# Values of the eleventh of sixteen groups of the second attention, projected between the FFN's gated product and its last product

## The chip, the cores and the metric

The kernel runs on one core of one Trainium2 chip. The metric is the device time of one execution in microseconds (us). The five engines of the core have queues of their own: PE (matrix products; PEld are its weight loads), DVE, ACT and POOL (elementwise work), and SP, which here only issues transfers (DMAs). An engine takes its instructions in the order in which the program has them. [...]

## What is computed

Four layers, each with a normalisation before it and a residual sum after it, on x of 32 sequences of 128 tokens with 256 features, all in float32:

```python
x = x + xattn_0(layernorm(x), ctx, ctx, mask)          # 16 heads of 16, masked
x = x + ffn_0(layernorm(x), w_gate, w_up, w_down)      # fake-quantised, 768 wide
x = x + xattn_1(layernorm(x), ctx, ctx, Wq, ..., beta) # 16 heads of 64
x = x + moe(layernorm(x), W1, b1, W2, b2, Wr, br)      # 8 experts of 1024, one per token
```

In the second layer every quantisation takes its scale from the largest magnitude of a whole tensor, so a step can't begin before the step ahead of it has ended for all tokens:

```python
x = act_qdq(x)
up = act_qdq(x @ lpbq_dequant(w_up).T)
gate = act_qdq(x @ lpbq_dequant(w_gate).T)
sig = fixed_qdq_u16(sigmoid(gate))
gate = act_qdq(gate * sig)
o = act_qdq(gate * up)            # the gated product
return o @ lpbq_dequant(w_down).T # the last product
```

In the third layer the values depend on the context alone, not on the layers before it:

```python
v = (value @ Wv + bv).reshape(b, value.shape[1], N_HEAD, VALUE_DIM)
out = einsum('bhqk,bkhd->bqhd', softmax(q k / 8), v)
```

## The kernel before

The tokens stand as 32 blocks of 128 (one sequence each). The stages follow each other: first attention, FFN, second attention, experts. Most stages are written with an order by hand: PE, DVE, ACT and POOL run their instructions as the source issues them; SP's order is the tile framework's, which also puts in every wait and decides from which instruction on a buffer is free.

*The second attention* goes through 16 groups of two blocks (G = 2). Each block has two units of eight heads, so a group is four units u = 0 to 3, and the loop over n runs 64 units. While unit n's probabilities are transposed (`transpose_c`, L1094) and multiplied by the values (`values_c`, L1109), unit n+1's scores are made (`scores_c`, L1052), and between these PE does the steps of the next group (`step`, L1000 and L1019): eight steps for its keys and queries, and four more for its values, two halves of 512 columns for each of two blocks. The constant NF (10) says for how many groups the values have been made beforehand. For such a group `values_of` (L1031) loads them from a DRAM tensor `v_d` with one transfer of 1024 KB. In the unit loop, `short = g + 1 < NF` chooses between two orders by hand: the short one issues eight steps over the four units of group g, the other one twelve (three per unit). So the units of groups 0 to 8 have the short order and those of groups 9 to 15 the long one.

*The values made beforehand.* These projections are set into the FFN, where PE has idle time. The pool `vf` holds the weights `wv_f` and three buffers `cf` for a block's transposed context (`load_v`, L678, 128 KB each from `ct_d`). `project_v(b, h, ps)` (L685) makes half h of block b with two matmuls of 512 columns (four records in the trace); `take_v` (L692, L693) copies the PSUM bank to a buffer `vs` and SP writes it to `v_d` (256 KB). Blocks 0 and 1 are made in the loop of up-projections. Then comes the gated product: a loop over 16 half-tiles s, with two ACT passes (L815, L818) and two DVE passes (L821, and `absmax` at L596) each, in which PE makes blocks 2 to 17; their banks are taken one round later. After this loop block 17 is taken, and the last loop (L826) makes blocks 18 and 19, both copied by ACT. The PSUM banks of this stage rotate over six, the buffers `vs` over five.

*Then the last product.* The global maximum is reduced (DVE L144, POOL L146), the scales s_o and k_o are worked out (DVE L834 to L839), and `quant_o(n)` quantises two blocks at a time: DVE makes int16 (L1245), ACT turns them back to float32 `oq` (L1247), and PE multiplies by `wdT` (L1265), 24 records in each of 16 rounds. After a round DVE adds x1, which SP has read back from DRAM (L1254, two buffers), and SP writes the sum x2 (L1272). `quant_o(n + 2)` stands ahead of round n's sum on DVE. SP also loads the weights of the attention here (L1277, L1279, 1024 KB each), and ACT issues the loads of small rows and biases (L857 to L870). The pools of this stage use space that the pools `vf` and `vp` (of `vs`) held.

Of the kernel before, what the change touches and what calls it, by code (L numbers as in the profile page):

```python
# [36 lines left out]
def tile_xattn_ffn_d2(  # L37
# [67 lines left out]
    toks_d = dram.tile([NC * P, 1], F32, name="toks_d")  # L105
    kacc_d = dram.tile([E, D], F32, name="kacc_d")

    NF = 10
    G = 2
    TG = G * P  # L110
    v_d = dram.tile([NF * G, P, D1], F32, name="v_d")

# [88 lines left out]
    with (  # L201
# [323 lines left out]
        with tc.manual_schedule(engines=by_hand):  # L525
            for n in range(-9, N + 8):
                b, k = divmod(n, KD)
# [67 lines left out]
    def absmax(n, t, i, r):  # L595
        nc.vector.tensor_reduce(  # L596
            amax[n][:, t, i : i + 1], r, AX.XY, ALU.max, apply_absolute_value=True
        )
# [4 lines left out]
    def half(r, i):  # L603
        return r[:, i * HM : (i + 1) * HM, :]
# [72 lines left out]
    def load_v(b):  # L677
        if b < NF * G:  # L678
            cfs[b] = vf.tile([P, KD, P], F32, tag="cf", name="cf", bufs=3)
            nc.sync.dma_start(out=cfs[b], in_=ct_d[b])  # L680

    def project_v(b, h, ps):

        for k in range(KD):
            nc.tensor.matmul(  # L685
                ps, lhsT=cfs[b][:, k, :], rhs=wv_f[:, k, h * 512 : (h + 1) * 512],
                start=(k == 0), stop=(k == KD - 1),
            )

    def take_v(b, h, ps, pool, copy):  # L690
        vs = pool.tile([P, 512], F32, tag="vs", name="vs")
        copy(vs, ps)  # L692
        nc.sync.dma_start(out=v_d[b, :, h * 512 : (h + 1) * 512], in_=vs)  # L693
# [3 lines left out]
    with (  # L697
# [44 lines left out]
        for t in range(NT):  # L742
# [5 lines left out]
            if t % 2:  # L748
                b, h = divmod(t // 2, 2)
# [25 lines left out]
    with (  # L775
        tc.tile_pool(name="bq", bufs=2, side="left") as ql,
        tc.tile_pool(name="ub", bufs=5, side="right") as ub,
        tc.tile_pool(name="vp", bufs=5, side="right") as vp,
        tc.tile_pool(name="b_v", bufs=6, space=PSUM) as pv,
        tc.manual_schedule(engines=by_hand),  # L780
    ):
        order = [*range(NT * 2 - KEPT, NT * 2), *range(NT * 2 - KEPT)]
        FU = 5

        def load_u(s):
            if s < NT * 2 and order[s] < NT * 2 - KEPT:
                n = order[s]
                ups[divmod(n, 2)] = ub.tile([P, HM, TB], F32, tag="ub", name="ub", bufs=FU)
                nc.sync.dma_start(
                    out=ups[divmod(n, 2)], in_=u_d[n].rearrange("p (m b) -> p m b", m=HM)  # L790
                )

        for s in range(KEPT + FU - 1):
            load_u(s)

        def take(s, h):

            if took:
                copy = nc.vector.tensor_copy if h and s % 2 else nc.scalar.copy
                take_v(1 + s, h, took[h], vp, copy)  # L800

        taken = []
        for s, n in enumerate(order):
            took, taken = taken, []
            for h in range(2):
                taken.append(pv.tile([P, 512], F32, tag="v", name="ps_vf"))
                project_v(2 + s, h, taken[h])
            load_v(5 + s)
            if s >= KEPT:
                load_u(s + FU - 1)  # L810
            t, i = divmod(n, 2)
            r = half(gates[t], i)
            u = ups[t, i]
            u16 = ql.tile([P, HM, TB], I16, tag="u16", name="u16")
            nc.scalar.activation(u16, u, AF.Copy, scale=i_u)  # L815
            take(s, 0)
            gs16 = ql.tile([P, HM, TB], I16, tag="gs16", name="gs16")
            nc.scalar.activation(gs16, r, AF.Copy, scale=k_s)  # L818
            take(s, 1)

            nc.vector.scalar_tensor_tensor(r, gs16, s_s, u16, ALU.mult, ALU.mult)  # L821
            absmax("o", t, i, r)
        took = taken
        for h in range(2):
            take(NT * 2, h)
        for b in range(2 + NT * 2, NF * G):  # L826
            for h in range(2):
                ps_v = pv.tile([P, 512], F32, tag="v", name="ps_vf")
                project_v(b, h, ps_v)
                take_v(b, h, ps_v, vp, nc.scalar.copy)  # L830
# [155 lines left out]
    def step(g, n):  # L986
# [3 lines left out]
        if "kT" not in s:  # L990
            if g >= NF:
                s["v"] = qkv.tile([P, G, D1], F32, tag="v", name="v")
# [36 lines left out]
    def values_of(g):  # L1029

        if g < NF:  # L1031
            groups_[g]["v"] = qkv.tile([P, G, D1], F32, tag="v", name="v")
# [541 lines left out]
    with tc.manual_schedule(engines=by_hand):  # L1574
# [16 lines left out]
        for n in range(N):  # L1591
            b, hf = divmod(n, 2)
# [4 lines left out]

            short = g + 1 < NF
            if short:
# [284 lines left out]
```

## Time and profile before

| | us |
|---|---|
| median of three runs (lowest, highest) | 1555.7 (1555.5, 1561.92) |
| the profiled execution: its time | 1557.21 |
| the profiled execution: span from first to last instruction | 1555.5 |
| mean granted clock of PE in it | 0.992 |
| gated product and values, from the last up-projection to PE's last projection | about 465 to 532.15 |
| last product of the FFN on PE | 538.73 to 624.18 |
| second attention, steps and units | 624.18 to about 1245 |
| experts | to 1555.5 |

The page gives busy times over the whole span. What a change in one stage is worth is read from that stage: from the order of events around it, and from the busy time of each engine in a stretch. Times in the trace count from the start of the span. Two kinds of idle time matter here: of PE between two products, and of a queue that waits for a transfer to land.

### The profile page before, as it was taken

Reading aid. Unit: us, or ns where it says so; the run is one execution under the profiler, and the core shown is the slowest. Engines: PE = TensorE matmul, PEld = TensorE weight load, DVE = VectorE, ACT = ScalarE, POOL = GpSimd, SP = SyncE. Lnnn points to the kernel's source line nnn. Section 1 sums busy time; section 2 is a strip of 40 time slices with the busy share of each in tenths; the row PEclk is TensorE's granted clock in tenths of the full one; section 3 lists DMA queues with packets and bytes.
Section 4 is the critical chain, followed back from the end, with each engine's and each line's share of the span. In section 5 each row is a group of like instructions: output and inputs, shape, how many; then the busy total and the mean of one; then the engine's idle time right before and its main releaser. Section 6 shows DMA issues by size and latency. Waiting matters only on the chain. (4 is left out here: it accounts for less than half of the span.)

```text
span 1555.5 us, 27850 instructions
## 1 busy us (share of the span) xinstructions
PE 1495.8 (96%) x9912; PEld 1109.1 (71%) x9912; DVE 945.6 (61%) x2290; ACT 821.3 (53%) x2425; POOL 455.5 (29%) x529
## 2 busy tenths in 40 slices
PE   8999999899998799999999999999999998999996
PEld 5656566444443388788888888777777667999996
DVE  7999998345999834456666666656566551333332
ACT  6878787345989732465566555454544421111111
POOL 6656664000000001223333333323233222232221
PEclk9999999999999999999999999999999999999998
DMA  7222211001437875213222321010102235251430
GB/s 242 69 86 83 66 35 46 14 5 74 159 123 257 292 206 168 85 55 55 55 55 56 60 59 60 16 26 23 21 19 64 55 106 202 101 170 50 166 104 12
DMA packets 84172, 139.99 MB, mean 90 GB/s; under 512 B 13098, under 2 KB 61245, under 8 KB 80448
## 3 DMA queue, kind: packets, MB, share of 16 engines
q1 hardware_dynamic: 74496, 125.16, 25.2%
q0 software_dynamic: 5568, 12.61, 2.8%
q8 instruction: 80, 1.31, 0.4%
q10 hardware_dynamic: 3968, 0.42, 0.4%
q14 instruction: 60, 0.49, 0.2%
HBM read 147.53 MB, written 45.77 MB: 124 GB/s over the span
## 5 line engine op out<-in xcount | busy, mean ns | idle before, releaser
L1071 ACT ACTIVATE pr_c<-sc_c,nmaxc 128x128 f32<-128x128 f32 x512 | 183.2, 384 | 194.1 <-DVE nmaxc L1062 137.9
L1083 POOL TENSOR_TENSOR pr_c<-pr_c,rsumc 128x512 f32<-128x512 f32 x64 | 92.8, 1449 | 279.4 <-DVE rsumc L1080 226.6
L1444 ACT ACTIVATE hT<-h_ps,w1s 128x128 f32<-128x128 f32 x156 | 48.1, 365 | 221.7 <-issue 141.5
L1010 DVE TENSOR_SCALAR qT<-ps_qk,bqk 128x256 f32<-128x256 f32 x128 | 61.8, 483 | 136.3 <-ACT kT L1006 135.6
L419 ACT ACTIVATE pr<-sc_a,nmaxa 128x128 f32<-128x128 f32 x512 | 140.1, 399 | 3.5 <-DVE nmaxa L410 3.5
L1000 PE MATMUL ps_qk<-cT,wk_s 128*128 128x256 f32 x512 | 140.3, 396 | 0.0
L1476 PE MATMUL y_d<-w2s,hT 128*128 128x256 f32 x576 | 133.3, 385 | 4.3 <-ACT hT L1444 4.3
L1435 PEld LDWEIGHTS h_ps<-xbT,w1s 128*128 128x128 f32 x1152 | 134.1, 192 | 1.7
L1435 PE MATMUL h_ps<-xbT,w1s 128*128 128x128 f32 x1152 | 134.6, 275 | 0.0
L1000 PE MATMUL ps_qk<-rT,wq_s 128*128 128x256 f32 x512 | 131.4, 379 | 0.0
L1476 PEld LDWEIGHTS y_d<-w2s,hT 128*128 128x128 f32 x576 | 108.7, 194 | 18.4 <-ACT hT L1444 4.5
L1122 PE MATMUL y_ps<-wo_s,oT 128*128 128x256 f32 x512 | 117.0, 382 | 0.0
L1071 ACT ACTIVATION_READ_ACCUMULATOR pr_c<-sc_c,nmaxc 128x1 f32 x512 | 114.0, 223 | 0.0
L1446 DVE TENSOR_SCALAR hT<-h_ps,w1s 128x128 f32<-128x128 f32 x132 | 40.1, 346 | 110.1 <-ACT hT L1444 110.1
L1000 PEld LDWEIGHTS ps_qk<-rT,wq_s 128*128 128x128 f32 x512 | 97.3, 190 | 13.2
L1122 PEld LDWEIGHTS y_ps<-wo_s,oT 128*128 128x128 f32 x512 | 94.7, 190 | 12.0 <-DVE pid L1721 0.4
L1000 PEld LDWEIGHTS ps_qk<-cT,wk_s 128*128 128x128 f32 x512 | 87.4, 189 | 18.8 <-issue 5.1
L1006 ACT ACTIVATE kT<-ps_qk,bqk 128x256 f32<-128x256 f32 x128 | 63.6, 498 | 57.4 <-PE ps_qk L1000 57.4
L1265 PE MATMUL ps_dn<-wdT,oq 128*128 128x256 f32 x384 | 85.1, 384 | 6.6 <-ACT oq L1247 6.6
L410 DVE TENSOR_REDUCE nmaxa<-sc_a 128x4 f32<-128x512 f32 x128 | 82.1, 683 | 11.6 <-PE sc_a L401 11.4
L1265 PEld LDWEIGHTS ps_dn<-wdT,oq 128*128 128x128 f32 x384 | 74.0, 193 | 17.7 <-ACT oq L1247 7.4
L609 PE MATMUL ps_mm<-xqT,wgT 128*128 128x512 f32 x192 | 83.8, 593 | 0.2 <-ACT xqT L641 0.2
(279 smaller groups left out, 2983.4 us busy)
## 6 DMA issues: line engine op xcount, KB each, us to landing
w1s<-in_W1b_dram SPq DMA_DIRECT2D x34, 1028.0 KB
w2s<-in_W_dram SPq DMA_DIRECT2D x34, 1024.0 KB
v_d<-vs SPq DMA_DIRECT2D x40, 256.0 KB
v<-v_d SPq DMA_DIRECT2D x10, 1024.0 KB
u_d<-u SPq DMA_DIRECT2D x12, 768.0 KB
ub<-u_d SPq DMA_DIRECT2D x12, 768.0 KB
w2e<-in_W_dram SPq DMA_DIRECT2D x8, 1024.0 KB
rows_d<-row SPq DMA_DIRECT2D x32, 256.0 KB
```

Of the source, the lines that this page charges most:

```text
L410: nc.vector.tensor_reduce(u["nmax"][:, r, :], u["scs"][r], AX.X, ALU.max, negate=True)
L419: nc.scalar.activation(u["pr"][:, r * HQ + j, :], u["scs"][r][:, j, :], AF.Exp, bias=u["nmax"][:, r, j : j + 1],)
L609: nc.tensor.matmul(ps, lhsT=wT[:, k, m * P : (m + 1) * P], rhs=xqT[:, k, t * TB : (t + 1) * TB], start=(k == 0), stop=(k == KD - 1),)
L1000: nc.tensor.matmul(ps[:, j, :], lhsT=w_[:, k, m * P : (m + 1) * P], rhs=src[:, k, :], start=(k == 0), stop=(k == KD - 1),)
L1006: nc.scalar.activation(s["kT"][:, m, :], ps[:, 0, :], AF.Identity, bias=bqk[:, 1, m : m + 1])
L1010: nc.vector.tensor_scalar(s["qT"][:, m, :], ps[:, 1, :], bqk[:, 0, m : m + 1], HD1**-0.5, ALU.add, ALU.mult,)
L1071: nc.scalar.activation(u["pr"][:, h, :], u["scs"][par][:, mm, :], AF.Exp, bias=u["nmax"][par][:, mm : mm + 1], accum_out=u["sums"][:, h : ...
L1083: eng.tensor_tensor(pr[:, j : j + 4, :], pr[:, j : j + 4, :], bc(rsum[:, j : j + 4], 2, P), ALU.mult,)
L1122: nc.tensor.matmul(t["y_ps"][:, :D], lhsT=t["oT"][:, m, :], rhs=wo_s[:, m, :], start=(m == 0), stop=(m == M1 - 1),)
L1265: nc.tensor.matmul(ps[:, j, :], lhsT=oq[:, m, j * P : (j + 1) * P], rhs=wdT[:, m, :], start=(m == 0), stop=(m == M0 - 1),)
L1435: nc.tensor.matmul(h_ps[:, c4, :], lhsT=wb[:, k * FF + c * P : k * FF + (c + 1) * P], rhs=xbT[:, k, :], start=(k == 0), stop=(k == KD - 1),)
L1476: nc.tensor.matmul(y_ps[:, :D], lhsT=hT[:, c, :], rhs=w2t[:, c, :], start=(c == 0), stop=(c == MF - 1),)
```

## The change

NF goes from 10 to 11. So the tensor `v_d` has 22 blocks, the last loop of the stage makes blocks 18 to 21 instead of 18 and 19, `values_of` loads group 10 from DRAM too, and the units of group 9, in which group 10 is prepared, have the short order. As blocks 20 and 21 have to be loaded, the loop over s loads block 20 in its last round (there `load_v(5 + s)` did nothing before, since 20 was no block to be made), and the last loop calls `load_v(b + 3)`, which loads block 21 while b is 18 and does nothing after that. Block 21 takes the buffer of block 18, and its transfer waits for that block's last matmul.

```diff
-    NF = 10
+    NF = 11
     G = 2
     TG = G * P
     v_d = dram.tile([NF * G, P, D1], F32, name="v_d")
...
         for h in range(2):
             take(NT * 2, h)
         for b in range(2 + NT * 2, NF * G):
+            load_v(b + 3)
             for h in range(2):
                 ps_v = pv.tile([P, 512], F32, tag="v", name="ps_vf")
                 project_v(b, h, ps_v)
                 take_v(b, h, ps_v, vp, nc.scalar.copy)
```

In the changed program every line from L827 on stands one lower.

## The prediction

> **What bounds the kernel now.** The page's first part says that PE is the engine to look at; it does not say where its free time is.
>
> ```profile
> PE 1495.8 (96%) x9912; PEld 1109.1 (71%) x9912; DVE 945.6 (61%) x2290; ACT 821.3 (53%) x2425; POOL 455.5 (29%) x529
> ```
>
> So I read two stages: the one that gives work away and the one that takes it. First the attention, by stretches that run from one group's second score product to the next group's (columns: stretch, its length, then PE, PEld, DVE, ACT, POOL busy, PE's clock, DMA share, GB/s).
>
> ```profile
> 893.51:929.92 36.41, 36.19 (x278) 30.63 (x277) 23.74 (x75) 22.06 (x86) 13.37 (x14) 1.00 0.24 60
> 929.92:966.32 36.40, 36.19 (x277) 30.61 (x277) 23.57 (x74) 21.84 (x86) 13.34 (x13) 1.00 0.27 56
> 966.32:1009.86 43.54, 43.32 (x293) 33.28 (x292) 26.98 (x82) 21.96 (x87) 15.26 (x15) 1.00 0.09 25
> 1009.86:1052.86 43.00, 43.00 (x293) 33.28 (x292) 26.10 (x79) 21.58 (x86) 13.25 (x13) 1.00 0.11 26
> 1052.86:1095.86 43.00, 43.00 (x293) 33.28 (x292) 26.11 (x79) 21.48 (x86) 12.96 (x13) 1.00 0.11 26
> ```
>
> A short group takes 36.4 us, a long one 43.0 (the first long one 43.54). PE is full in both, the others are not and the DMAs have room, so a group's length is its PE work. Here PE work that goes away is time that goes away.
>
> Then the timeline of PE, DVE and ACT where the FFN's last product begins.
>
> ```profile
> 518.13 14.02 PE L685 MATMUL ps_vf<-wv_f,cf 128*128 128x512 f32 x32 [0.66 <-DMA cf<-ct_d]
> 538.73 61.44 PE L1265 MATMUL ps_dn<-wdT,oq 128*128 128x256 f32 x276 [6.58 <-ACT oq L1247]
> ...
> 535.76 0.16 DVE L839 TENSOR_TENSOR k_o<-i_o,s_u 128x1 f32<-128x1 f32 x1
> 536.04 1.95 DVE L1245 TENSOR_SCALAR o<-r,k_o 128x1536 int16<-128x1536 f32 x2
> ...
> 531.25 0.59 ACT L692 COPY vs<-ps_vf 128x512 f32<-128x512 f32 x1 [0.67 <-DMA v_d<-vs]
> 533.18 0.59 ACT L692 COPY vs<-ps_vf 128x512 f32<-128x512 f32 x1 [1.34 <-DMA v_d<-vs]
> 537.10 1.57 ACT L1247 ACTIVATE oq<-o,s_o 128x1536 f32<-128x1536 int16 x1 [3.34 <-DVE o L1245]
> ```
>
> PE ends block 19 at 532.15 and then has nothing for 6.58 us, until the maximum, the scales, the int16 pass (1.0 us of the 1.95 for two) and oq (1.57) are done. The clock pays for this idle time:
>
> ```profile
> 532.15:538.73 6.58, 0.01 (x1) 0.01 (x1) 5.09 (x10) 2.22 (x3) 0.55 (x2) 0.73 0.90 304
> 538.73:545.81 7.08, 7.08 (x25) 6.00 (x26) 1.00 (x1) 1.41 (x1) 0.01 (x1) 0.77 0.90 299
> 545.81:550.99 5.18, 5.18 (x25) 4.56 (x24) 1.62 (x2) 1.57 (x1) 0.00 (x0) 1.00 0.81 49
> ```
>
> The first round of the last product takes 7.08 us at a clock of 0.77, the next one 5.18 at 1.00: 1.90 us lost. So this hole costs 6.58 of idle time and 1.90 behind it.
>
> **The change part by part.**
>
> *Removed from the attention.* The units of group 9 go from the long order to the short one: 43.00 - 36.41 = **6.59 us** off PE's path. The 0.54 us by which the first long group is longer goes along to group 10 and is no gain. Checked from the other side: four value steps are 16 records, and 32 records took 14.02 us, so 16 take 7.01; the short order gives 0.4 of it back. I take 6.59, bounds 6.59 to 7.01. The four DVE copies that go too are worth nothing beside a full PE. Added: one load of 1024 KB from v_d by SP while group 9 runs, as for groups 1 to 9; in those stretches the DMAs are a quarter busy, and the load has a group's 36 us to land. I cost it at nothing; were it late, unit 40's value product would wait for it.
>
> *Added to the FFN: PE.* Blocks 20 and 21 are four half projections of 1.75 us (14.02 / 8), 7.01 us, right behind block 19: from 532.15 to 539.16, if nothing holds them up. What could: (a) Their context. SP loads block 20 when block 17 is made (eight halves run from 518.13, so 17 ends at 525.1), block 21 when block 18 is made (528.6); each has 7 us until it is used, and the worst load here was used 7.6 us after its issue, 0.66 late, while 768 KB reads ran beside it, of which none are left now. (b) PSUM: with six banks, block 20's first half takes the bank of block 17's first half, which ACT emptied at 528.55 to 529.1. (c) The copies. With five vs buffers a copy waits until the write five before it has landed: 531.25 and 533.18 are such waits, each about 2.1 us after SP's issue of that write (529.15, 531.02). The next writes are issued from 531.43 to 532.92, some 0.5 us apart; at 2.1 us plus a backlog of 0.3 us for each (256 KB take about 0.8 us at 340 GB/s, an estimate from the 304 GB/s of the stretch above at its share of 0.90) they land between 533.6 and 536.5. PE ends the four halves at 533.9, 535.7, 537.4 and 539.2, so copies wait for PE and not the reverse.
>
> *The wait that comes in its place.* In the order of the changed program the first int16 pass (DVE, L1246 there) has a wait for PE, as it has before: its tile lies in space of the pool of the projections, so it waits for the last of them. Before, that was over at 532.15, nearly four us ahead of k_o. Now it ends at 539.16, three us behind k_o (535.92). Behind this instruction stand the second int16 pass and then everything of DVE; ACT has only the last copy (539.2 to 539.8) ahead of oq. So: int16 539.25 to 540.25, oq 540.3 to 541.87, first matmul of the last product at about 541.9 in place of 538.73: **+3.2 us**. PE's hole shrinks from 6.58 to 2.7 us.
>
> *The clock.* The trace has two other holes of that size: 2.69 us ahead of the transposes at 642.14, and 2.50 at 475.37. Stretches 639 to 642 and 642 to 646 both show a clock of 1.00. Only the holes of 6.58 and of 4.31 us (ahead of 1304.17) show it at half. So I take it as kept: **-1.9 us**; bounds -1.9 and 0.
>
> *Added: DMAs.* Four writes of 256 KB and two loads of 128 KB on SP's queue, 1.25 MB, about 3.9 us at 340 GB/s. Queued behind them are the attention's weights: the first waited until 538.38 for all writes of v_d, and now waits until about 542.6 (last copy 539.8, then a write). ACT's bias loads wait for the same. They are needed at 624 only, but the sums of x1 stand among them:
>
> ```profile
> SPq L1277 <- DMA bqk<-in_L_xattn_bq_dram: 8.1, 1, 8.1
> ...
> 561.55 0.69 DVE L1271 TENSOR_TENSOR x1r<-ps_dn,x1r 128x512 f32<-128x512 f32 x1 [8.94 <-PE ps_dn L1265]
> ...
> 563.26 1.57 ACT L1247 ACTIVATE oq<-o,s_o 128x1536 f32<-128x1536 int16 x1 [5.52 <-DVE o L1245]
> ```
>
> The line names PE, but round 2's matmuls had ended at 556.2: the sum waited five us more for x1, which SP issued at 556.50. The int16 pass for round 5 stands behind it, so oq(5) was ready at 564.83, and PE needed it at 538.73 + 7.08 + 4 x 5.18 = 566.5: 1.7 us of cover. In the changed program SP writes the first x2 ahead of the third weight, not behind it, and reads x1 back ahead of the last weight. Both ends: all of it 4.2 us later against a PE 1.3 us later eats the cover and stalls PE by 4.2 - 1.3 - 1.7 = 1.2 us; the new order takes 1024 KB (3 us) out of the way twice and stalls nothing. I take 0, bounds 0 and 1.2.
>
> *Sum.* -6.6 + 3.2 - 1.9 = **-5.3 us** on a span of 1555.5: 1550.2. The profiled execution took 1557.21, 1.7 more than its span, which would be 1551.9; the median of the runs, 1555.7, is 1.5 below that execution, and becomes **1550.4**.
>
> **The rivals.**
>
> *A, the clock is lost again.* The mean clock is 0.52 in 535 to 540 and 0.80 in 540 to 545, so it was at half from 535.2 to 542.0; 0.53 in 1303 to 1306 and 0.60 in 1306 to 1311 put the second such time at 1303.2 to 1310.0. It fell 3.0 and 3.3 us into the holes. For: 2.7 is only 0.3 short of that. Against: the two holes of 2.5 and 2.7. Then the 1.9 isn't won: 1552.3.
>
> *B, the clock is won elsewhere too.* Ahead of the experts PE is idle from 1299.86 to 1304.17, the clock fell at 1303.2, and 16 records took 6.59 us that take 3.45 at 5.18 / 24 each: 3.1 us. Both half-speed times last 6.8 us and their starts are 768 us apart, which is 112.5 times 6.83: all four edges lie on a grid of 3.41 us. If the clock is judged on that grid, the hole held nearly a whole step (1299.8 to 1303.2); 5.3 us earlier, from 1294.6 to 1298.9, the edge at 1296.4 cuts it into 1.8 and 2.5, and the clock stays. Time 1550.4 - 3.1 = 1547.3. Against: if the fall just follows 3.0 to 3.3 us of idle time, nothing changes. [...]
>
> *C, slower: the chain through x2 and x1.* An x1 buffer is read again only when its x2 has landed: 547.82 to 556.50 to 561.55, 13.7 us, where two rounds of PE take 10.4. With 1.25 MB more ahead of it and bias loads that held SP's queue for 8.1 us, round 2's sum may come so late that PE is paced by transfers. It decides from a landing at 564.5 on (561.55 + 1.7 + 1.3), and the kernel is slower than before from 569.8 on. At a landing 12 us later than before (573.5) the stall is 9 us: 1559.4. For: 0.8 to 1.0 DMA share from 532 to 560. Against: the new order of SP's queue.
>
> *D, the attention gives nothing back,* because the short order was fast only beside early groups: 1555.7 + 1.3 = 1557.0. Against: nine groups run it at the same length.
>
> **How the numbers follow.** Forecast 0.52, A 0.15, B 0.20, C 0.08, D 0.05. What a measurement here tells from no change is about 0.5%, 7.8 us: faster is below 1547.9, slower above 1563.5. B is faster (0.20), and a little of the forecast with the 7.01 and a lucky clock (0.03): 0.23. Slower needs C at twice the price worked out or something unseen: 0.06. The rest, 0.71, is the same. The range: below, 1555.7 - 7.0 - 1.9 + 3.2 - 3.1 = 1546.9; above, A with the stall of 1.2 is 1553.5, and up to C's beginning 1555.
>
> **What would show it.** Right: group 9's stretch at 36.4 us; eight halves and then four more on PE without a gap, the first L1266 matmul at 541 to 543, released by oq, its first round at 5.2 us and a clock of 1.00; round 2's sum before 564. Wrong: a hole of over 3.4 us ahead of the last product, a wait of PE for oq in its rounds 3 to 8, or a group 9 longer than 37 us.

## The result, and the profile after

| | before | after |
|---|---|---|
| median of 20 runs each, us | 1559.09 | 1555.61 |
| lowest to highest, us | 1555.5 to 1563.14 | 1553.3 to 1558.16 |
| the profiled execution: time, span, us | 1557.21, 1555.5 | 1556.43, 1554.7 |

The ratio is 0.9979 (95% interval 0.9972 to 0.9986): the changed kernel is 3.3 us faster (2.2 to 4.4), about 0.2%. The forecast was 1550.4, a gain of 5.3. The three runs of before that it started from had their median at 1555.7; 20 runs have it at 1559.09. So of the 5.2 us between 1550.4 and 1555.6 some 3 are the starting point, and 2 are the size of the change. The kernel scatters by 7.6 us from run to run; the last point of the causes below says what that is seen to come from.

The attention first. These stretches of the changed kernel run from one group's second score product to the next group's, as those shown of before: their length, then PE, PEld, DVE, ACT, POOL busy, PE's clock, DMA share, GB/s.

```profile
937.40:973.81 36.41, 36.19 (x278) 30.62 (x277) 23.58 (x74) 21.85 (x86) 13.34 (x13) 1.00 0.34 59
973.81:1010.22 36.41, 36.19 (x278) 30.62 (x277) 23.82 (x75) 22.06 (x86) 13.40 (x14) 1.00 0.21 57
1010.22:1053.76 43.54, 43.32 (x294) 33.27 (x293) 26.91 (x82) 21.96 (x87) 15.23 (x15) 1.00 0.12 26
```

The stretch in the middle, the changed one, took 43.54 before; the first long group, 43.54, is now one later, where 43.00 stood. The scores of unit 37 start 7.49 us later than before (973.81 against 966.32), those of unit 45 only 0.90 (1053.76 against 1052.86): 6.59 us are gone, the forecast's figure to the digit.

Then the timeline of PE, DVE and ACT around the start of the FFN's last product.

```profile
524.53 15.72 PE L685 MATMUL ps_vf<-wv_f,cf 128*128 128x512 f32 x36 [0.46 <-ACT vs L692]
537.19 0.16 DVE L840 TENSOR_TENSOR k_o<-i_o,s_u 128x1 f32<-128x1 f32 x1
540.29 1.95 DVE L1246 TENSOR_SCALAR o<-r,k_o 128x1536 int16<-128x1536 f32 x2 [2.94 <-PE ps_vf L685]
541.34 3.04 ACT L1248 ACTIVATE oq<-o,s_o 128x1536 f32<-128x1536 int16 x2 [0.42 <-DVE o L1246]
542.97 64.11 PE L1266 MATMUL ps_dn<-wdT,oq 128*128 128x256 f32 x288 [2.72 <-ACT oq L1248]
...
545.39 5.16 ACTq L866 DMA_DIRECT2D bvT<-in_L_xattn_bv_dram  x1
...
553.27 1.57 ACT L1248 ACTIVATE oq<-o,s_o 128x1536 f32<-128x1536 int16 x1 [8.89 <-issue]
...
563.54 0.69 DVE L1272 TENSOR_TENSOR x1r<-ps_dn,x1r 128x512 f32<-128x512 f32 x1 [6.60 <-DMA x1r<-x_d]
```

The new wait is the third line's: k_o is there at 537.35, and the int16 pass stands until PE's last projection at 540.25, for 2.94 us. PE's hole is 2.72 us, the forecast's 2.7. The first matmul comes 4.24 us later than before (538.73); 1.4 of this was there by 388, where the first projection of this execution already starts late (388.44 against 387.03), so in this execution the change itself delays the start by 2.8 us.

The stretches of that hole and of the two rounds behind it, columns as above. The second line is one window of the 3.41 us grid that the prediction's rival B works out; it is used further below.

```profile
540.25:542.97 2.72, 0.00 (x0) 0.00 (x1) 1.97 (x3) 2.21 (x3) 0.00 (x0) 1.00 0.75 258
540.37:543.78 3.41, 0.81 (x4) 0.73 (x5) 2.70 (x3) 2.98 (x3) 0.00 (x0) 1.00 0.71 231
542.97:550.14 7.17, 7.17 (x25) 6.04 (x26) 1.00 (x1) 1.42 (x1) 0.23 (x1) 0.76 0.90 295
550.14:555.32 5.18, 5.18 (x25) 4.56 (x24) 1.62 (x2) 1.57 (x1) 0.00 (x0) 1.00 0.82 92
```

The first round takes 7.17 us at a clock of 0.76, as before (7.08 at 0.77), though the hole ahead of it is 2.4 times shorter. The 1.9 us of the clock were not won here.

### The profile page after: what moved, and what is told of

Read it like the earlier page. It is cut to its first block, busy times and chain, and to the rows that moved or that the text cites. A ratio compares the mean times of both kernels' runs of the same rounds, so it can differ in the third digit from the quotient of the medians.

```text
span 1554.7 us, 27869 instructions
## 1 busy us (share of the span) xinstructions
PE 1498.9 (96%) x9912; PEld 1111.4 (71%) x9912; DVE 942.5 (61%) x2286; ACT 824.2 (53%) x2429; POOL 456.2 (29%) x529
## 5 line engine op out<-in xcount | busy, mean ns | idle before, releaser
L685 PE MATMUL ps_vf<-wv_f,cf 128*128 128x512 f32 x176 | 78.7, 598 | 6.6 <-ACT vs L692 3.5
```

The source lines that it names most:

```text
L685: nc.tensor.matmul(ps, lhsT=cfs[b][:, k, :], rhs=wv_f[:, k, h * 512 : (h + 1) * 512], start=(k == 0), stop=(k == KD - 1),)
```

## The experiments

Every kernel was timed beside the kernel before, in 4 to 12 executions each; a gain is what the ratio lacks of 1, times 1559 us. Line numbers in the profiles of edited kernels stand a few higher.

**The two halves apart.** One constant for the FFN's side, one for the attention's:

```diff
-    NF = 11
+    NF, NA = 11, 10      # e1: eleven made, ten used; in e2: 10, 11
...
-            if g >= NF:
+            if g >= NA:
...
-        if g < NF:
+        if g < NA:
...
-            short = g + 1 < NF
+            short = g + 1 < NA
```

e1 makes blocks 20 and 21 and doesn't use them:

> The FFN's part of the change alone: blocks 20 and 21 are projected and written, but the attention makes group 10's values itself as before and never reads them. Theory (the int16 pass waits for the last projection, and in the shorter hole of 2.7 us the clock of PE is still lost in part of the executions): the last product starts 2.8 us later as in the changed kernel's trace, so 0.9 to 2.8 us slower than before, about 2. Rival (the FFN's part costs nothing but the loss comes later, in the attention's start or the experts): within 0.5 us of before.

e2 leaves them out, and loads the values of group 9 a second time for group 10:

> The attention's part alone: group 9's units have the short order and group 10's values are loaded, but blocks 20 and 21 are not projected; group 10 uses the values of group 9 (its output is another one than the reference's). Theory: 6.6 us faster than before, all of it in the units of one group, a hole of 6.58 us ahead of the last product as before. Rival (part of the 6.6 us is given back later): 3 to 5 us faster.

The FFN's half alone: ratio 1.0014 (1.0003 to 1.0024), 2.2 us slower. The attention's half alone: 0.9954 (0.9941 to 0.9967), 7.2 us faster. The attention's half is worth the 6.6 within its interval (5.1 to 9.2). For the FFN's half the forecast had +3.2 and -1.9, which is 1.3; the interval (0.5 to 3.7 us) holds that and the 2.8 without the clock, so the time alone doesn't decide. Together the halves are 5.0 us faster, the whole 3.3; with 2 us of interval on each half that is no contradiction, and no confirmation to better than 2 or 3 us. The stretches of e1 decide: the hole is the same, and the clock is lost too.

```profile
540.55:543.27 2.72, 0.00 (x1) 0.00 (x0) 1.97 (x3) 2.21 (x3) 0.00 (x0) 1.00 0.67 230
543.27:550.45 7.18, 7.18 (x25) 6.03 (x26) 1.01 (x2) 1.42 (x1) 0.20 (x1) 0.76 0.90 294
```

**What the start waits for.** The pool of the int16 tiles goes to the other side of SBUF, away from the projections' pool:

```diff
-        tc.tile_pool(name="bdn", bufs=2, side="right") as dn,
+        tc.tile_pool(name="bdn", bufs=2, side="left") as dn,
```

> The whole change, with the pool of the last product on the other side of SBUF, where it no longer overlaps the projections' pool by 924 bytes; its first int16 pass then has no wait for PE. Theory: the int16 passes run right behind k_o beside the last projections, the last product starts within 0.6 us of the last projection, no hole and no loss of clock there: 7 to 8.5 us faster than before. Rival (the start is held by something else: copies, transfers): like the changed kernel, 3 to 4 us faster than before.

0.9963 (0.9950 to 0.9976), 5.8 us faster than before. The wait for PE is gone: the int16 pass runs at 537.98, right behind k_o. But PE's next wait stands in the same place. First the list of PE's waits (engine, line, what it waited for: us, times, longest), then the timeline:

```profile
PE ps_dn L1266 <- ACT vs L692: 2.2, 1, 2.2
```

```profile
537.98 1.95 DVE L1246 TENSOR_SCALAR o<-r,k_o 128x1536 int16<-128x1536 f32 x2
539.03 1.58 ACT L1248 ACTIVATE oq<-o,s_o 128x1536 f32<-128x1536 int16 x1 [0.92 <-DVE o L1246]
540.52 0.56 ACT L692 COPY vs<-ps_vf 128x512 f32<-128x512 f32 x1
...
540.98 1.57 ACT L1248 ACTIVATE oq<-o,s_o 128x1536 f32<-128x1536 int16 x1
542.46 0.57 ACT L692 COPY vs<-ps_vf 128x512 f32<-128x512 f32 x1
...
543.08 2.34 PE L1266 MATMUL ps_dn<-wdT,oq 128*128 128x256 f32 x7 [2.20 <-ACT vs L692]
```

The PSUM banks of the last product, to which PE writes `ps_dn`, are those of the projections (`ps_vf`), so the first matmul waits for the copy of the last projection, here 2.20 us; and this copy now stands on ACT behind both passes of oq, which runs earlier, until 543.03. The first matmul came at 543.08, no sooner than in the changed kernel, and the hole of 2.20 us lost the clock again (first round 7.23). The time, 5.8 (3.7 to 7.8), lies between the two forecasts; as the start is no earlier than in the changed kernel, nothing at this place explains more than that kernel's 3.3, and the two intervals overlap.

**The hole kept warm.** Six matmuls of 256 columns without use, behind the last projection:

```diff
+        ps_w = pv.tile([P, 512], F32, tag="v", name="ps_w")
+        for _ in range(6):
+            nc.tensor.matmul(
+                ps_w[:, :D], lhsT=ident, rhs=wdT[:, 0, :], start=True, stop=True
+            )
     vfp.__exit__
```

> The whole change, with six idle matmuls of 256 columns on PE behind the last projection (2.6 us, read by nobody), so that PE works through the hole of 2.7 us. Theory (the clock is lost in that hole in a good part of the executions): first round of the last product always 5.2 us, 4.5 to 5.7 us faster than before, that is 1 to 2 us faster than the changed kernel. Rival (the clock survives a hole of 2.7 us in nearly all executions): same as the changed kernel, 3 to 4 us faster than before.

0.9983 (0.9972 to 0.9994), 2.7 us faster than before, which is no better than the changed kernel. The stretch of the first round shows that the clock was kept, and the timeline what followed:

```profile
545.80:551.27 5.47, 5.47 (x25) 4.84 (x26) 0.99 (x1) 1.40 (x1) 0.20 (x1) 1.00 0.87 273
```

```profile
548.31 5.04 ACTq L871 DMA_DIRECT2D bvT<-in_L_xattn_bv_dram  x1
...
556.06 3.04 ACT L1253 ACTIVATE oq<-o,s_o 128x1536 f32<-128x1536 int16 x2 [8.86 <-issue]
...
557.69 2.64 PE L1271 MATMUL ps_dn<-wdT,oq 128*128 128x256 f32 x11 [1.28 <-ACT oq L1253]
```

The first round takes 5.47, 1.7 less. Then PE waits 1.28 us for the third oq. On ACT it stands behind the issues of the eight small loads, of which the fourth held the queue for 5.04 us. The same issues are in the changed kernel (545.39, 5.16 us); there the slow first round covers them. A kept clock uncovers this wait, and most of its gain is gone again: 1.7 less 1.28 is 0.4.

This profile has a second loss, which lies ahead of the edit: one projection waited 2.06 us for its context.

```profile
522.23 20.84 PE L685 MATMUL ps_vf<-wv_f,cf 128*128 128x512 f32 x48 [2.06 <-DMA cf<-ct_d]
```

So the last product starts 7.7 us behind the start of k_o there (545.80 against 538.13), in the changed kernel 5.8; the profiled execution took 1561.02 us, the median of e4 is 1557.12.

**Both releases away.** The pool on the left as above, the projections on five banks in place of six, and the last product's three banks moved to those that the projections don't use (the pool `b_sp` only takes up space ahead of them):

```diff
-        tc.tile_pool(name="b_v", bufs=6, space=PSUM) as pv,
+        tc.tile_pool(name="b_v", bufs=5, space=PSUM) as pv,
...
+        tc.tile_pool(name="b_sp", bufs=3, space=PSUM) as psp,
         tc.tile_pool(name="b_dn", bufs=3, space=PSUM) as pdn,
```

> As the run with the last product's pool on the other side, and its PSUM banks apart too: five banks instead of six for the projections, and the last product's three outside them, so that its first matmul needs no copy of a projection. Theory: the last product starts within 0.5 us of the last projection (3.1 us behind k_o), the clock is kept, but round 2's oq stands on ACT behind the issues of the bias loads, which wait for the last write of v_d: PE waits for it 1.5 to 2.5 us in round 2. In all 5.5 to 7 us faster than before. Rival (ACT's queue does not matter): 7.5 to 9 us faster, no wait in round 2.

0.9962 (0.9951 to 0.9974), 5.9 us faster. In the timeline of PE the last product follows the last projection without a hole, and the wait for the third oq stays, at 1.06 us against the 1.5 to 2.5 expected:

```profile
534.77 8.32 PE L685 MATMUL ps_vf<-wv_f,cf 128*128 128x512 f32 x19
542.92 10.52 PE L1268 MATMUL ps_dn<-wdT,oq 128*128 128x256 f32 x48
554.51 5.66 PE L1268 MATMUL ps_dn<-wdT,oq 128*128 128x256 f32 x25 [1.06 <-ACT oq L1250]
```

**The small loads off ACT.** Their five issuing lines go to POOL, in the kernel of e5 (e6), in that of e4 (e7), in the kernel before (e9) and in the changed kernel (e10); in e11 one of the eight goes, and in e12 all go to SP. e8 is e6 with six idle matmuls more in each of two earlier holes (ahead of the first transposes of x, near 278 us, and of the second group of the attention, near 641 us).

```diff
-    nc.scalar.dma_start(out=wr_s, in_=wr.rearrange("(k p) e -> p k e", p=P))
+    nc.gpsimd.dma_start(out=wr_s, in_=wr.rearrange("(k p) e -> p k e", p=P))
...
-        nc.scalar.dma_start(out=rows[n], in_=v.partition_broadcast(P))
+        nc.gpsimd.dma_start(out=rows[n], in_=v.partition_broadcast(P))
```

e6, on e5:

> As the run before it, with the eight loads of small rows and biases issued by POOL in place of ACT. Theory: no wait in round 2; 7.5 to 9 us faster than before, and 1.5 to 2.5 us faster than the same kernel with these loads on ACT. Rival (ACT's queue does not matter): the same as that kernel.

e7, on e4:

> The changed kernel with six idle matmuls in the hole ahead of the last product, and the bias loads issued by POOL. Theory (the clock is worth 1.9 us there, but the wait for oq behind ACT's bias loads ate it in the run with the idle matmuls alone): the first round takes 5.2 to 5.5 us, no wait in round 2, 5 to 6 us faster than before. Rival (that run gained nothing for another reason): 2.5 to 3.5 us faster, as that run.

e8, on e6:

> The kernel with pools and banks apart and the bias loads on POOL, with six idle matmuls more in each of two other holes of PE: ahead of the FFN's first transposes (at about 278) and ahead of the transposes at the attention's start (at about 643). Theory (holes of 2.5 to 2.9 us lose the clock in most executions, 1.2 us behind the first, 1.6 on average behind the second): 2 to 3 us faster than the same kernel without them, 9.5 to 11.5 faster than before. Rival (the clock is mostly kept in such holes, as forecast): no faster than the same kernel without them.

e9, on the kernel before:

> The kernel before, with the eight small loads (router weights, biases, rows) issued by POOL and not by ACT; values of ten groups made beforehand. The runs that moved these loads came out some 10 us faster than expected, and their traces put 8.0 us of it at the very end: POOL's closing pair of semaphore count and drain takes 2.25 + 8.40 us in every kernel in which POOL issues indirect transfers alone, and 0.68 + 1.95 us in the three in which it issued plain ones too. Theory: that has nothing to do with the change of NF, and the loads on ACT's queue hold up no product here, so this kernel is 8.0 us faster than before (ratio 0.995, closing drain 1.95 us). Rival: the gain came from ACT's queue and the projections of group 10 in front of it; then this kernel is within 1 us of before, and the closing drain is 8.4 us.

e10, on the changed kernel:

> The changed kernel with the same eight loads issued by POOL, and nothing else. Theory: 8.0 us off the end of the program, and the hole of 2.7 us ahead of the last product still loses the clock (first round 7.1 us), so nothing is gained by the free ACT queue itself: 11.3 us faster than the kernel before (ratio 0.9928), 3 to 4 us faster than the kernel before with the loads on POOL (the change is worth the same in both settings). Rival, ACT's queue alone cost the changed kernel what the forecast missed, 2 us: 13.3 us faster (0.9915), with a first round of 7.1 us all the same.

e11, one load of the eight:

> The changed kernel with one single small load (the query biases, 4 KB) issued by POOL, the other seven by ACT as before. Theory, any plain transfer on POOL's queue shortens the closing drain, to 1.95 us: 11.3 us faster than the kernel before (ratio 0.9928). Rival, the drain goes by how many such transfers POOL has issued: one of eight gives about 1 us, so 4.3 us faster (0.9972). Second rival, the gain lies in ACT's freed queue: closing drain 8.4 us, 3.3 us faster (0.9979).

e12, all eight on SP:

> The changed kernel with all eight small loads issued by SP, ahead of the attention's weights: neither ACT nor POOL issues a plain transfer any more. One plain load on POOL left the closing drain at 8.48 us, eight made it 1.95. Theory: it goes by whether ACT issues any transfer at all; then this kernel's drain is 1.95 us and it is 11 to 12 us faster than the kernel before, as with the loads on POOL (ratio 0.9925). Rival: it goes by how many plain loads POOL has issued; then the drain is 8.40 us, and the time is that of the changed kernel (0.9979), or up to 1 us above it if the loads on SP's queue hold x1 up.

| kernel | median, us | ratio to before (95%) | POOL's closing count and drain, us |
|---|---|---|---|
| changed kernel | 1555.61 | 0.9979 (0.9972 to 0.9986) | 2.25 + 8.40 |
| e5: both releases away | 1555.05 | 0.9962 (0.9951 to 0.9974) | 2.25 + 8.40 |
| e6: e5, loads on POOL | 1544.02 | 0.9900 (0.9882 to 0.9918) | 0.68 + 1.95 |
| e7: e4, loads on POOL | 1545.57 | 0.9910 (0.9893 to 0.9927) | 0.68 + 1.95 |
| e8: e6, two more holes filled | 1542.00 | 0.9883 (0.9863 to 0.9903) | 0.68 + 1.95 |
| e9: before, loads on POOL | 1548.73 | 0.9924 (0.9911 to 0.9937) | 0.68 + 1.95 |
| e10: changed, loads on POOL | 1547.80 | 0.9918 (0.9905 to 0.9931) | 0.68 + 1.95 |
| e11: changed, one load on POOL | 1555.67 | 0.9967 (0.9955 to 0.9980) | 2.27 + 8.48 |
| e12: changed, loads on SP | 1556.08 | 0.9977 (0.9967 to 0.9987) | 2.25 + 8.40 |

e6 and e7 came out some 7 to 9 us faster than expected, and 8.0 us of this has nothing to do with the last product. Behind the last scatter of the result POOL closes with a semaphore count and a drain; the raw events of the trace give their lengths in the table's last column. With the eight small loads on POOL the pair is 8.0 us shorter (2.63 against 10.65), at the very end, where nothing covers it. e9 shows it in the kernel before too (2.63); in e11 one such load was not enough (10.75), and in e12 an ACT queue without any load did not do it (10.65). Why POOL closes sooner then stays open. e9's gain of 11.3 to 12 us is 3 more than the pair. The granted clocks on record account for most of this: 0.9952 on average over e9's five executions, 0.9903 over the eleven of before timed beside them, which is 15 and 30 us at half clock (an estimate, twice the missing share times the span, as the clock that was granted after a fall is 0.50 in the stretch from 646.18 shown further below). Up to 10 of these 15 us lie behind PE's last product, where they cost nothing (in the profile of before, half clock from 1545.52 to the end); the other 5 or so are worth two to three us of PE's work. So e9's executions seem to have lost the clock less often on the way. That moving the loads did this is not shown.

What is about the change: in e6 PE waits for nothing in the whole last product (e5: once, 1.06 us), and in e7 the hole is filled, the first round takes 5.47, and no oq is late. So ACT's queue was what held the third oq. In the times little of this can be seen: e7 and e10, which differ by the idle matmuls alone, are 1.2 us apart with overlapping intervals. The price of the clock, 1.7 us in the first round, rests on the stretches. e10 against e9 is the change in a kernel whose ACT queue is free: 0.9 us faster, with intervals of about 2 us on either side, so it can be told neither from the 3.3 measured here nor from nothing. e10 lost the clock (its first round took 7.17). e12, with the loads on SP, kept it in a hole of the same 2.72 us:

```profile
539.25:542.67 3.42, 1.94 (x5) 0.57 (x3) 1.44 (x2) 2.09 (x4) 0.00 (x0) 1.00 0.91 324
542.67:546.08 3.41, 2.17 (x10) 1.94 (x11) 1.53 (x2) 2.66 (x2) 0.20 (x1) 1.00 0.70 220
543.91:549.40 5.49, 5.49 (x25) 4.86 (x26) 1.00 (x2) 1.42 (x2) 0.20 (x1) 1.00 0.57 81
```

The first two stretches are windows of this execution's grid of 3.41 us, counted from the times at which its own clock fell: 283.25, 477.81 and 645.07. An edge, at 542.67, cuts the hole (541.19 to 543.91) into 1.5 and 1.2 us, and either window has about 2 us of PE's work in it. In the changed kernel's execution the window 540.37 to 543.78, shown above, held 2.6 us of the hole and 0.81 of work, and the clock fell at its end. Same hole, other phase, other outcome.

e8 beats both kernels, by 1.2% (1.0 to 1.4) over before: 8.0 of its 18 us are the closing pair; how the other 10 divide among the change, the free start, the clock and whatever gave e9 its 3 us, no run separates. It is 2.0 us below e6, from which it differs by the idle matmuls alone; the two intervals overlap.

## Why the prediction was wrong, step by step

- *Removed from the attention, -6.59.* Right: 6.59 in the profile, 7.2 (5.1 to 9.2) alone. Group 9's units took the 36.41 us of the other short groups, so rival D is out, and no product of PE waited for group 10's load.
- *The wait that comes in its place, +3.2.* Right in place, cause and size: 2.8 in the changed kernel's profile, and 2.8 to 3.3 over the five profiles with this wait (in after, e1, e10, e11 and e12 the first matmul starts 5.8 to 6.2 us behind the start of k_o, in before 2.96). What the step didn't see is that a second release, of the banks through ACT's copy, holds the same start once the first is gone (e3).
- *The clock, -1.9: this step failed.* It read from two holes of the trace of before (2.69 and 2.50 us, both at 1.00) that a hole of 2.7 us is short enough. Those two were one execution's luck, as was a third hole of that trace which the step passed over (2.86 us, from 277.81, clock kept). Over the 14 profiles, holes of 2.5 to 2.9 us in four places: ahead of the first transposes of x the clock fell in 10 of 12, at the projections near 474 us in 5 of 11, ahead of the attention's second group in 11 of 13, ahead of the last product in 4 of 5. The profiles without the change always lost it in the hole of 6.5 us (3 of 3: before, e2, e9). So the change wins the clock in perhaps one execution of five, and the term is about -0.4 in place of -1.9 (an estimate from few profiles). Rival A, given 0.15, was the likeliest case: it says 1552.3, a gain of 3.4, and 3.3 was measured. With the terms as the runs have them, -6.6 + 3.1 - 0.4 is a gain of 3.9 (an estimate), inside the measured 2.2 to 4.4. None of the prediction's three signs of being wrong came; of its signs of being right the one that failed is the first round at 5.2 us.
- *Added: DMAs, 0.* Right for the time: round 2's sum came at 563.54, before the 564 named, and PE waited for no oq after the first. But the step followed only SP's queue to x1. ACT's own queue, with the loads' issues ahead of the third oq, was the tighter one. With a kept clock it stalls PE by 1.28 (e4) or 1.06 (e5). So even with the clock the forecast's -1.9 would have shrunk to some 0.4 to 0.8. The trace of before had shown the queue: that oq was ready at 549.59, 1.4 us ahead of PE's third round at 550.99.

```profile
540.11 5.05 ACTq L865 DMA_DIRECT2D bvT<-in_L_xattn_bv_dram  x1
548.02 1.57 ACT L1247 ACTIVATE oq<-o,s_o 128x1536 f32<-128x1536 int16 x1 [7.88 <-DVE o L1245]
```

- *Rival B, by the grid.* Its grid is right: in each of the 14 profiles all falls lie on one grid of 3.41 us, to 0.01 us. Its criterion isn't: a window needs not be idle throughout. PE's busy share of each window at full clock, worked out for all 14 profiles up to 1530 us: all 52 windows with a share up to 0.42 were followed by a fall, 3 of 12 between 0.43 and 0.49, and none of some 80 between 0.50 and 0.76. (Later, where PE runs out of work, 9 of 10 up to 0.42 were; e12 has the exception, 0.41 at 1539.4.) This is read from the traces: no run set the phase of the grid by intent, but e12 and the changed kernel show the same hole at two phases. By this the hole of 6.6 us costs the clock at any phase (an estimate; it did in 3 of 3), and one of 2.7 us with full work around it keeps it only where an edge leaves less than about 1.9 us of it on either side (3.41 us less 0.45 of it), 30% of all phases (an estimate: of 3.41 us of phase, 1.04 lie so).
- *Rival B's own hole*, ahead of the experts, did not keep the clock in the changed kernel's profile: it fell at 1304.95, and a fall somewhere between 1288 and 1313 is in all 14. But it was at half for one window there, in before for two, so that 16 products took 5.41 us against 6.59; the hole was 0.46 shorter too (3.85 against 4.31). That is 1.6 us of the 3.1 that B named.
- *Rival C* did not come: nothing in the changed kernel's rounds waits for x1 on PE.
- *The starting point.* The profiled execution of before, and two of the three runs shown, lie at the lower end of the 20. In that profile none of the holes near 278, 474 and 641 us lost the clock; the changed kernel's lost it at the first and the third. The third as an example, by stretches: in before an edge cut the hole (639.45 to 642.14), and the window behind the edge had 2.21 us of work; in after 2.4 of its 2.84 us fell into one window with 1.01 of work, and 6.82 us at half clock follow.

Before:

```profile
640.93:644.35 3.42, 2.21 (x22) 1.88 (x23) 2.63 (x6) 0.53 (x2) 1.54 (x1) 1.00 0.11 32
```

After:

```profile
642.77:646.18 3.41, 1.01 (x5) 0.55 (x3) 0.90 (x3) 3.17 (x16) 0.65 (x1) 1.00 0.29 77
646.18:653.00 6.82, 6.38 (x28) 5.20 (x29) 3.94 (x10) 1.51 (x8) 1.46 (x2) 0.50 0.00 0
```

From unit 0's scores to unit 5's the changed kernel took 45.36 us there, before 42.21: 3.15 lost. The loss at the first hole is the 1.4 already seen, and the experts' hole gives the 1.6 back. So the two profiles add up: -6.59 + 2.8 + 1.4 + 3.15 - 1.6 is -0.8, the difference of the spans, while the medians differ by 3.5.

## What to carry to other kernels

Clock losses differed from execution to execution here (the mean granted clock of 17 executions of before lay between 0.987 and 0.993): read them from several profiles, and price a hole by the work left in the windows it can fall into, not by its length against one lucky row. Where a wait is removed, list every release of the same start (tile space, PSUM banks, the engine's own queue) and what each would be without the others; here the banks held the start as late as the tile space did (543.08 against 542.97), and ACT's queue held the third round by 1.1 to 1.3 us as soon as PE was faster. And look at the instructions behind the last product of work too: here the closing count and drain of POOL were worth more than the whole change (8.0 us against 3.3).

## What was not expected of the hardware

POOL's closing semaphore count and drain took 10.65 us in the eight kernels without any plain load on POOL, 10.75 in the one with one (e11), and 2.63 in the five with eight. And over the 14 profiles, ahead of 1530 us, PE's clock fell after each of the 52 windows of 3.41 us with up to 0.42 of it at work, after 3 of 12 between 0.43 and 0.49, and after none of some 80 between 0.50 and 0.76.
